# A two-layer graph network: the start laid out anew, the last eight tiles of layer 1 in a loop of their own, and q's writes and stack load moved to another sub-step

## The chip, the cores and the metric

The kernel runs on one core of a Trainium2 chip. The metric is the device time of one execution in microseconds (us); runs of the same kernel are compared by their median. Times inside the kernel come from the profile of one execution. A core has five engines that work side by side, each through its own instructions in order: TensorE (PE in the profile; its weight loads are listed as PEld), VectorE (DVE), ScalarE (ACT), GpSimd (POOL) and SyncE (SP), which here only issues DMAs. GpSimd issues DMAs too, in order with its computing.

## What is computed

x is (16, 1024, 256) in float32: 16 graphs of 1024 nodes. adj is (16, 1024, 1024) of int32, 0 or 1 in this input, about 3% ones, with ones on the diagonal. There are two layers, each with a layer norm, a ReLU and a residual:

```python
# layer 0: 8 heads of 32, D = 256
h = maximum(layernorm(x), 0)
Q, K, V = h @ Wq.T + bq, h @ Wk.T + bk, h @ Wv.T + bv      # split into heads
scores = where(adj == 0, -inf, Q K^T / sqrt(32))           # (b, head, 1024, 1024)
x = x + (softmax(scores) V) @ Wo.T + bo
# layer 1
h = maximum(layernorm(x), 0)
e_k = leaky_relu(einsum(h * a_k, h), 0.2)                  # k = 0..3
scores = where(adj == k + 1, e_k, ...), -9e15 elsewhere    # adj is 0 or 1 here: only e_0
x = x + softmax(scores) @ h
```

## The kernel before

**Tiles and steps.** The unit of work is a tile of 128 rows (nodes) of one graph; b is the graph, called a batch below, t = 0..7 the tile in it. Layer 0 handles one tile for all 8 heads in one step of the main loop (L736); step s is the pair (b, t) = divmod(s, 8). The steps overlap: in step s TensorE computes the scores of tile s (class Attend, L378), the output of tile s - 1, the projections of tile s + 9 or so (class Piece, L182, LEAD = 9 steps ahead) and layer 1 of tile s - 9 (class Edges, L547, LAG = 9 steps behind). Keys, queries and values of a graph must be whole before its first scores, and layer 1 needs all 8 tiles of a graph's layer 0, so the distances are a little over one graph. The loop ran 138 steps: 128 with scores, the last ten (s = 128 to 137) with only layer 1 and what is left of layer 0.

**The order is written out by hand** (`tc.manual_schedule()`, L699): each engine executes its instructions, and each queue its DMAs, in the order in which the program text issues them. Waits between engines are put in by the framework where a tile is written before it is read, or where its buffer is used again; work on the DRAM scratch arrays is ordered by regions in the same way. Each step has eight sub-steps h = 0..7, one per head, and the lines `if h == 3:` say which work goes where.

**One head.** Scores s = q·k (L423) are two matmuls of 128x512; VectorE adds the mask and takes the maximum (L435); ScalarE makes the Exp (L443). The probabilities must then be transposed for the product with V. Heads 2, 3, 6 and 7 are turned by TensorE (L543) and copied by ScalarE (L544). Heads 0, 1, 4 and 5 (BY_BLOCKS) go another way: VectorE transposes 32x32 blocks (L364, into the buffers "blocks"), and SP's DMAs, four of 128 KB per head, place the blocks in the turned order (L369, into "pT"). combine(0) (L478) multiplies the turned probabilities of heads 0 to 3 by V at sub-step 7, combine(1) those of heads 4 to 7 at sub-step 3 of the next step.

**Queries and keys.** Each projection (L261) is split in two halves, a high one by ScalarE (high, L277) and the remainder by VectorE (split, L282). Keys are written to a DRAM scratch array kd twice (write_keys, L309, once by SP and once by GpSimd), queries to qd (write_queries, L303: two DMAs of 256 KB on SP, which write each half twice). From there they are read back stacked, so that one matmul of full depth does the product of the halves. The query stack of one tile is one load of 512 KB into "qt" (load_queries, L390, on SP; two buffers). The key stacks are one load of 512 KB per head (load_key, L344), by SP for graph 0 and by GpSimd for the others, spread over the steps t = 7 and t = 0 at fixed places (KEY_STEPS).

**What SP's queue does in one step** of the main loop, in order: at h = 0 the first write of keys (L309) and the four placings of layer 1's tile; at h = 1 the second write of keys and the load of the next tile's stack (L390); at h = 2 and h = 3 the placings of heads 0 and 1; at h = 6 layer 1's output store (L619), the placings of head 4 and layer 0's result for later (L504); at h = 7 the placings of head 5 and q's two writes for tile s + 8 (L303).

**What GpSimd does** beside its DMAs: the mask (L403) of the next tile from adj (load L394, 512 KB, issued at h = 4), norms (norm_of, L143: a chain of 18 small operations, L152 to L168), small copies.

**Layer 1 of one tile** (Edges): scores e (L565, four matmuls of 128x512 into the score bank `sides[1]`), maximum with mask (L579), leak (L587), Exp (L591), block transposes and placings (by the same L364 and L369, into "pT1"), the product with h (gather, L609, 64 small matmuls in two halves), the store (L619). Its buffers (`sel`, `pT1`, `ha`, `x1b`) are single.

**The start.** Ahead of the loop the first graph's rows are loaded as two pieces of four tiles, normalised, turned, projected (q and k), written to qd and kd and read back, and the values computed; the first piece of graph 1 is begun. Small biases and the four weights are loaded first (L104 to L140), on SP, and each weight is turned by TensorE as it is loaded.

**After the loop** a test finds out whether some adj was over 1; then a general layer 1 (`layer_1_of_kinds`) would run. It does not run on this input.

Of the kernel before, what the change touches and what calls it, by code (L numbers as in the profile page):

```python
# [17 lines left out]
P = 128  # L18
# [24 lines left out]
def gnn_kernel(  # L43
# [59 lines left out]
    a_t = const.tile([P, NC, N_KINDS], F32, name="a_t")  # L103
    with nc.allow_non_contiguous_dma(reason="a few hundred elements, once"):  # L104
        nc.sync.dma_start(out=bq_t, in_=bq.rearrange("(c p) -> p c", p=P))
        nc.sync.dma_start(out=bk_t, in_=bk.rearrange("(c p) -> p c", p=P))
        for k, a in enumerate((a_0, a_1, a_2, a_3)):
            nc.sync.dma_start(out=a_t[:, :, k], in_=a.rearrange("(c p) o -> p (c o)", p=P))
    bv_t = const.tile([P, D], F32, name="bv_t")
    bo_t = const.tile([P, D], F32, name="bo_t")  # L110
    for i in range(2):
        nc.sync.dma_start(
            out=bv_t[:, i * P : (i + 1) * P].rearrange("p (r d) -> p r d", r=2),
            in_=bv.rearrange("(r i d) -> i r d", i=2, r=2)[i].partition_broadcast(P),
        )
    nc.sync.dma_start(out=bo_t, in_=bo.partition_broadcast(P))

    def transposed_weight(w, name):

        rows = work.tile([P, NC, D], F32, tag="p", name=f"{name}_rows", bufs=4)  # L120
        nc.sync.dma_start(out=rows, in_=w.rearrange("(c p) f -> p c f", p=P))
        wt = const.tile([P, NC, D], F32, name=name)
        tr = ps_tr.tile([P, 4, P], F32, tag="tr", name=f"{name}_tr")
        for fc in range(NC):
            for oc in range(NC):
                nc.tensor.transpose(tr[:, fc * NC + oc, :], rows[:, oc, fc * P : (fc + 1) * P], ident)
        if name == "wvT":
            for fc in range(NC):
                nc.vector.tensor_copy(
                    wt[:, fc].rearrange("p (i r d) -> p r i d", i=2, r=2),  # L130
                    tr[:, fc * NC : (fc + 1) * NC].rearrange("p r (i d) -> p r i d", i=2),
                )
        else:
            nc.vector.tensor_copy(wt.rearrange("p c f -> p (c f)"), tr.rearrange("p c f -> p (c f)"))
        return wt

    wqT = transposed_weight(wq, "wqT")
    wkT = transposed_weight(wk, "wkT")
    wvT = transposed_weight(wv, "wvT")
    woT = transposed_weight(wo, "woT")  # L140


    def norm_of(mv):  # L143
# [4 lines left out]
        def place(name, dtype=F32):  # L148
            return small.tile([P, 4], dtype, tag=name, name=name)[:, :n]

# [19 lines left out]

    def stats_place(n):
        return small.tile([P, 4, nc.vector.BN_AGGR_DIM], F32, tag="mv", name="mv")[:, :n, :]

# [5 lines left out]

    qds, kds, vs, keysets = {}, {}, {}, {}  # L180

    class Piece:  # L182
# [66 lines left out]
        def project(self, which, oc):  # L249
            wT, bias = ((wkT, bk_t), (wqT, bq_t))[which]  # L250
            b, w = self.b, self.n * P
# [67 lines left out]
        def values(self):  # L319
# [3 lines left out]
            for t in range(self.n):  # L323
                ps = (late, early, brief)[t % 3]
                self.vproj = ps
                for i, hT in enumerate((self.hTm, self.hT)):
                    for fc in range(NC):
                        nc.tensor.matmul(
                            ps[:, i * P : (i + 1) * P],
                            lhsT=hT[:, fc, t * P : (t + 1) * P],  # L330
                            rhs=wvT[:, fc, i * P : (i + 1) * P],
                            start=(fc == 0),
# [45 lines left out]
    class Attend:  # L378
# [111 lines left out]
        def output(self):  # L490
            self.y = late
            for g in range(NC):
                nc.tensor.matmul(
                    self.y, lhsT=self.oT[:, g, :], rhs=woT[:, g, :], start=(g == 0), stop=(g == NC - 1)
                )
# [195 lines left out]
    def edges_of(s):  # L691
        s -= LAG
        return Edges(*divmod(s, NT)) if 0 <= s < B * NT else None

# [4 lines left out]
    with tc.manual_schedule():  # L699
        first = [Piece(0, 0, 4), Piece(0, 4, 4)]  # L700
        piece_was = Piece(1, 0)
        for piece in (*first, piece_was):
            piece.load(nc.sync)
        for piece in (*first, piece_was):
            piece.stats()
            piece.normed()
        now, piece_next = attend_of(0), piece_of(0)
        nxt = attend_of(1)
        now.load()
        now.flag()  # L710
# [23 lines left out]

        gone = was = None
        for s in range(B * NT + LAG + 1):  # L736
            b, t = divmod(s, NT)
# [8 lines left out]
            for h in range(HEADS):  # L746
# [66 lines left out]
                if h == 1:  # L813
# [64 lines left out]
            edge_was, edge = edge, edge_nxt  # L878
            piece_was, piece = piece, piece_nxt

# [51 lines left out]
```

## Time and profile before

| | us |
|---|---|
| runs | 3287.58, 3294.10, 3294.34 |
| median of the runs | 3294.1 |
| the profiled execution | 3310.77 |
| its span, first to last instruction | 3309.0 |
| mean granted clock of TensorE in it | 0.979 |

The profiled execution is 0.5% longer than the median of the runs. Some of the costliest groups of its page, with how often each occurred and the mean time of one:

| line, engine, what | count | busy us | mean ns |
|---|---|---|---|
| L435 VectorE, mask and maximum of a head's scores | 1024 | 1233.6 | 1205 |
| L443 ScalarE, Exp | 1024 | 1178.4 | 1151 |
| L423 TensorE, scores | 2048 | 797.3 | 471 |
| L478 TensorE, probabilities times V | 16384 | 561.0 | 283 |
| L364 VectorE, block transposes | 512 | 632.2 | 1235 |
| L403 GpSimd, mask | 128 | 467.0 | 3648 |

and of its list of DMAs, with the median time from the issue to the landing:

| DMA | count | KB each | us to landing |
|---|---|---|---|
| pT from blocks, SP (L369) | 2560 | 128 | 3.5 |
| qt from qd, SP (L390) | 128 | 512 | 5.5 |
| adj, GpSimd (L394) | 127 | 512 | 4.8 |
| qd from halves, SP (L303) | 240 | 256 | 3.2 |
| k from kd, GpSimd (L344) | 120 | 512 | 7.0 |
| kd from halves, SP (L309) | 240 | 128 | 3.8 |

How to read it: busy times of matmuls overlap (matmuls are pipelined), so the mean of one is not its time alone. An arrow names what ended a wait. A line such as `1611.66 8.02 SPq L369 DMA_DIRECT2D pT<-blocks x8` of a timeline is: start in the span, length, engine or queue, line of the program, operation, output<-input, and how many instructions were put together; a bracket at its end is the wait inside it. In a row of a table by windows, the columns after the length are TensorE, its weight loads, VectorE, ScalarE, GpSimd (busy us, number of instructions), then the granted clock, the DMA engines' busy share and GB/s.

### The profile page before, as it was taken

What the parts mean: (1) busy time and instruction counts of PE and PEld (TensorE: products, weight loads), DVE (VectorE), ACT (ScalarE), POOL (GpSimd) and SP (SyncE); (2) the same over time, 40 slices, a digit from 0 to 9 for tenths busy, and PEclk for the clock granted to TensorE, in tenths of its full rate; (3) what the DMA queues carried; (4) which work ended last, traced back from release to release, by engine and by line L of the source; (5) the groups of instructions that cost most, each with busy time, mean ns of one, the idle gap of its engine ahead of it and who ended that gap; (6) DMA issues with size and microseconds to landing.
All of it is one profiled execution on the core that took longest, in us unless ns stands there. A gap on an engine that the chain in (4) does not pass through costs nothing. (4 is left out here: it accounts for less than half of the span.)

```text
span 3309.0 us, 98026 instructions
## 1 busy us (share of the span) xinstructions
PE 3080.0 (93%) x36018; PEld 2239.0 (68%) x36018; DVE 2802.7 (85%) x5111; ACT 2458.4 (74%) x4829; POOL 1735.3 (52%) x3902
## 2 busy tenths in 40 slices
PE   4888999999999999999999999999999999998997
PEld 2666767777676767767677677776766676676653
DVE  2887989989898989989899888989988899898963
ACT  2887878778787877878778777878777788787750
POOL 2555555555555555555555555555555555555531
PEclk9898999999999999999999999999999999999999
DMA  5777787877878787787878878787787877877642
GB/s 187 219 232 227 235 262 221 269 225 235 264 221 267 225 254 241 223 261 228 255 229 240 245 229 253 228 261 237 229 257 218 250 235 231 252 231 242 197 136 70
DMA packets 747063, 762.93 MB, mean 231 GB/s; under 512 B 71280, under 2 KB 692080, under 8 KB 746576
## 3 DMA queue, kind: packets, MB, share of 16 engines
q1 hardware_dynamic: 678288, 542.21, 55.3%
q0 software_dynamic: 65088, 210.16, 19.9%
q8 instruction: 290, 4.75, 0.6%
q10 hardware_dynamic: 3200, 4.19, 0.3%
q14 instruction: 197, 1.61, 0.1%
HBM read 252.98 MB, written 167.77 MB: 127 GB/s over the span
## 5 line engine op out<-in xcount | busy, mean ns | idle before, releaser
L435 DVE CUSTOM_DVE_ANT_0 p<-s,neg 128x1024 f32<-128x1024 f32 x1024 | 1233.6, 1205 | 150.6 <-issue 120.5
L443 ACT ACTIVATE p<-p,nmx 128x1024 f32<-128x1024 f32 x1024 | 1178.4, 1151 | 221.2 <-DVE nmx L435 219.7
L423 PE MATMUL s<-k,qt 128*128 128x512 f32 x2048 | 797.3, 471 | 21.8 <-DVE nmx L435 9.8
L478 PE MATMUL acc<-pT,v 128*32 128x128 f32 x16384 | 561.0, 283 | 112.3 <-DMA pT<-blocks 110.7
L544 ACT COPY pT<-trp 128x512 f32<-128x512 f32 x1024 | 543.8, 582 | 162.6 <-PE trp L543 151.9
L403 POOL TENSOR_SCALAR neg<-adj 128x1024 bf16<-128x1024 int32 x128 | 467.0, 3648 | 359.3 <-ACT neg L415 358.9
L364 DVE STREAM_TRANSPOSE blocks<-p 128x1024 f32<-128x1024 f32 x512 | 632.2, 1235 | 0.1
L478 PEld LDWEIGHTS acc<-pT,v 128*32 128x32 f32 x16384 | 472.1, 114 | 196.8 <-issue 119.4
L543 PE MATMUL trp<-ident,p 128*128 128x128 f32 x4096 | 534.2, 274 | 0.2 <-ACT pT L544 0.2
L543 PEld LDWEIGHTS trp<-ident,p 128*128 128x128 f32 x4096 | 481.0, 141 | 74.0 <-ACT pT L544 3.6
L609 PE MATMUL acc<-h,pT 128*32 128x256 f32 x8192 | 509.9, 383 | 12.5 <-DMA pT<-blocks 11.8
L565 PE MATMUL s<-h1T,ha 128*128 128x512 f32 x1024 | 482.8, 595 | 0.5 <-ACT h1T L522 0.5
L423 PEld LDWEIGHTS s<-k,qt 128*128 128x128 f32 x2048 | 331.1, 192 | 155.0 <-issue 107.7
L609 PEld LDWEIGHTS acc<-h,pT 128*32 128x32 f32 x8192 | 246.6, 110 | 228.5 <-issue 78.0
L462 POOL COPY wide<-rec 128x256 f32<-128x256 f32 x128 | 51.0, 398 | 573.3 <-DVE rec L460 573.3
L309 POOL DMA_DIRECT2D kd<-halves x240 | 169.6, 707 | 238.6 <-DVE halves L282 230.6
L579 DVE CUSTOM_DVE_ANT_0 sel<-s,neg 128x1024 f32<-128x1024 f32 x128 | 156.8, 1225 | 146.2 <-PE s L565 146.2
L565 PEld LDWEIGHTS s<-h1T,ha 128*128 128x128 f32 x1024 | 175.3, 191 | 130.0 <-issue 128.6
L591 ACT ACTIVATE sel<-sel,nmx 128x1024 f32<-128x1024 f32 x128 | 145.5, 1137 | 70.8 <-DVE rec L616 64.9
L443 ACT ACTIVATION_READ_ACCUMULATOR p<-p,nmx 128x1 f32 x1024 | 193.7, 189 | 0.0
L472 ACT COPY recT<-acc 128x256 f32<-128x256 f32 x128 | 47.8, 373 | 176.7 <-PE acc L468 176.7
L261 PEld LDWEIGHTS acc<-hT,wkT 128*128 128x128 f32 x960 | 119.5, 195 | 76.1 <-issue 46.9
(106 smaller groups left out, 4008.3 us busy)
## 6 DMA issues: line engine op xcount, KB each, us to landing
pT<-blocks SPq DMA_DIRECT2D x2560, 128.0 KB, 3.5
qt<-qd SPq DMA_DIRECT2D x128, 512.0 KB, 5.5
adj<-in_adj POOLq DMA_DIRECT2D x127, 512.0 KB, 4.8
qd<-halves SPq DMA_DIRECT2D x240, 256.0 KB, 3.2
k<-kd POOLq DMA_DIRECT2D x120, 512.0 KB, 7.0
kd<-halves SPq DMA_DIRECT2D x240, 128.0 KB, 3.8
kd<-halves POOLq DMA_DIRECT2D x240, 128.0 KB, 3.6
xb<-in_x POOLq DMA_DIRECT2D x128, 128.0 KB, 3.0
```

Of the source, the lines that this page charges most:

```text
L309: queue.dma_start(out=kds[self.b][oc, :, :, twice, self.cols], in_=halves.rearrange("p (w n) -> p w n", w=2),)
L364: nc.vector.transpose(blocks.rearrange("p b j q -> p j b q"), p)
L403: nc.gpsimd.tensor_scalar(self.neg, self.adj, 0.0, MASKED, ALU.is_equal, ALU.mult)
L423: nc.tensor.matmul(self.ps[:, cols], lhsT=self.qt[:, h, :], rhs=keysets[self.b][h][:, cols], start=True, stop=True,)
L435: nc.vector.tensor_tensor_reduce(out=p, in0=sides[h in (3, 5, 7)], in1=self.neg, scale=-SCALE, scalar=FLOOR, op0=ALU.add, op1=ALU.min, acc ...
L443: nc.scalar.activation(p, p, AF.Exp, bias=nmx, scale=-1.0, accum_out=self.sums[:, h : h + 1])
L478: nc.tensor.matmul(sums_place[r * HD : (r + 1) * HD, g * P : (g + 1) * P], lhsT=vs[self.b][:, j, place_of(h) : place_of(h) + HD], rhs=self ...
L543: nc.tensor.transpose(tr[:, j, :], p[:, jj * P : (jj + 1) * P], ident)
L544: copy(pT[:, half * 4 : half * 4 + 4, :], tr)
L565: nc.tensor.matmul(self.e[:, cols], lhsT=self.ha[:, c, :], rhs=h1Ts[self.b][:, c, cols], start=(c == 0), stop=(c == NC - 1),)
L579: nc.vector.tensor_tensor_reduce(out=self.sel, in0=self.e, in1=masks[self.b, self.t], scale=-1.0, scalar=3e38, op0=ALU.add, op1=ALU.min, a ...
L609: nc.tensor.matmul(sums_place[a * HD : (a + 1) * HD, :], lhsT=self.pT[:, j, a], rhs=h1s[self.b][:, j, :], start=(j == 0), stop=(j == NT - 1),)
```

## The change

**The start.** The rows of x are loaded first, the weights after them (in the order wk, wq, wv, wo), then the first piece of graph 1, the first adj, the biases and the next piece, all by SP. The statistics of the eight tiles of graph 0 go through one chain of norm_of (its places lie in one tile, "many", as the small tiles hold four columns). The weights are turned after the rows are normalised. All key projections of both pieces come before the query projections, and the eight key loads are issued as soon as the keys are written, ahead of q's writes and of the first stack load; the first mask and the second adj come after these. The values use the two rotating PSUM tiles of the transposes.

**The end.** The main loop ends with step 128. Layer 1's last eight tiles are computed in a loop of their own, in which both score halves of the next tile stand ahead of the gather of the tile before the one that is placed; these tiles alternate between the two score banks and use buffers that layer 0 no longer needs.

**The step.** write_queries moves from h = 7 of step s to h = 3 of step s + 1 (`piece_gone`), and load_queries of the next tile from h = 1 to h = 3, right behind it; both stay on SP. There they now stand behind the placings of head 1; before, the stack stood ahead of the placings of head 0, and q's writes behind those of head 5.

The diff, cut (the bodies of load_biases and of the weight turns are the old lines in a function; `wvT` and the like became `weights["wvT"]`):

```diff
--- before.py
+++ after.py
@@ -101,24 +101,32 @@
...
+    def load_biases():
+        with nc.allow_non_contiguous_dma(reason="a few hundred elements, once"):
+            nc.sync.dma_start(out=bq_t, in_=bq.rearrange("(c p) -> p c", p=P))
+            nc.sync.dma_start(out=bk_t, in_=bk.rearrange("(c p) -> p c", p=P))
...
+    weight_rows = {}
+
+    def load_weights():
+        for w, name in ((wk, "wkT"), (wq, "wqT"), (wv, "wvT"), (wo, "woT")):
+            weight_rows[name] = work.tile([P, NC, D], F32, tag="p", name=f"{name}_rows", bufs=4)
+            nc.sync.dma_start(out=weight_rows[name], in_=w.rearrange("(c p) f -> p c f", p=P))
+
+    def transposed_weight(name):
+
+        rows = weight_rows[name]
         wt = const.tile([P, NC, D], F32, name=name)
...
-    wqT = transposed_weight(wq, "wqT")
-    wkT = transposed_weight(wk, "wkT")
-    wvT = transposed_weight(wv, "wvT")
-    woT = transposed_weight(wo, "woT")
...
         def place(name, dtype=F32):
-            return small.tile([P, 4], dtype, tag=name, name=name)[:, :n]
+            if n <= 4:
+                return small.tile([P, 4], dtype, tag=name, name=name)[:, :n]
+            places.append(name)
+            return many[:, len(places) * n - n : len(places) * n].bitcast(dtype)
+
+        places = []
+        if n > 4:
+            many = work.tile([P, D], F32, tag="ot", name="many", bufs=1)
 
...
     def stats_place(n):
+        if n > 4:
+            return work.tile([P, n, nc.vector.BN_AGGR_DIM], F32, tag="oT", name="mv", bufs=1)
         return small.tile([P, 4, nc.vector.BN_AGGR_DIM], F32, tag="mv", name="mv")[:, :n, :]
...
         def write_queries(self):
-            for oc, halves in self.queries:
+            while self.queries:
+                oc, halves = self.queries.pop(0)
                 nc.sync.dma_start(
                     out=qds[self.b][self.first, oc].rearrange("p u w n -> p u (w n)"),
                     in_=halves.unsqueeze(1).to_broadcast([P, 2, 2 * P]),
...
             for t in range(self.n):
-                ps = (late, early, brief)[t % 3]
+                ps = late if self.n == 1 else ps_tr.tile([P, D], F32, tag="tr", name="vproj")
                 self.vproj = ps
...
-        def __init__(self, b, t):
+
+
+        def __init__(self, b, t, last=False):
             self.b, self.t = b, t
             self.rows = slice(t * P, (t + 1) * P)
+            self.side = sides[t % 2 if last else 1]
+            self.tags = {"sel": ("p", 4), "pT1": ("pT", 7)} if last else {}
+            if last and t % 2:
+                self.tags |= {"ha": ("hT", 1), "x1b": ("x1", 1)}
+
+        def buffer(self, tag, shape):
+            tag, bufs = self.tags.get(tag, (tag, 1))
+            return (ptp if tag in ("pT", "pT1") else work).tile(shape, F32, tag=tag, name=tag, bufs=bufs)
...
         def prepare(self):
-            self.ha = work.tile([P, NC, P], F32, tag="ha", bufs=1)
+            self.ha = self.buffer("ha", [P, NC, P])
...
-            self.e = sides[1]
+            self.e = self.side
...
         def softmax_max(self):
-            self.sel = work.tile([P, N], F32, tag="sel", bufs=1)
...
         def load_nodes(self):
-            self.x1 = work.tile([P, D], F32, tag="x1b", bufs=1)
+            self.x1 = self.buffer("x1b", [P, D])
...
         def place_blocks(self):
-            self.pT = placed(self.blocks, ptp.tile([P, N], F32, tag="pT1", name="pT1", bufs=1))
+            self.pT = placed(self.blocks, self.buffer("pT1", [P, N]))
...
@@ -690,7 +713,7 @@
 
     def edges_of(s):
         s -= LAG
-        return Edges(*divmod(s, NT)) if 0 <= s < B * NT else None
+        return Edges(*divmod(s, NT), s >= (B - 1) * NT) if 0 <= s < B * NT else None
...
@@ -698,42 +721,54 @@
 
     with tc.manual_schedule():
         first = [Piece(0, 0, 4), Piece(0, 4, 4)]
-        piece_was = Piece(1, 0)
-        for piece in (*first, piece_was):
+        piece_was, piece_next = Piece(1, 0), piece_of(0)
+        now, nxt = attend_of(0), attend_of(1)
+        for piece in first:
             piece.load(nc.sync)
-        for piece in (*first, piece_was):
-            piece.stats()
+        load_weights()
+        piece_was.load(nc.sync)
+        now.load()
+        load_biases()
+        piece_next.load(nc.sync)
+        mv = stats_place(NT)
+        for piece in first:
+            for t in range(piece.n):
+                stats_of(piece.x[:, t, :], mv[:, piece.first + t, :])
+        r, shift = norm_of(mv)
+        for piece in first:
+            piece.norm = tuple(a[:, piece.first : piece.first + piece.n] for a in (r, shift))
             piece.normed()
-        now, piece_next = attend_of(0), piece_of(0)
-        nxt = attend_of(1)
-        now.load()
-        now.flag()
-        now.mask()
-        nxt.load()
-        piece_next.load()
-        piece_next.stats()
+        for name in ("wkT", "wqT", "wvT", "woT"):
+            weights[name] = transposed_weight(name)
+        piece_was.stats()
         for piece in first:
             piece.turn()
-        for piece in first:
-            for which in range(2):
+        for which in range(2):
+            for piece in first:
                 for oc in range(NC):
                     piece.project(which, oc)
                     piece.high()
                     piece.split()
+            if which == 0:
+                for h in range(HEADS):
+                    load_key(0, h)
+        now.load_queries()
+        piece_was.normed()
+        now.flag()
+        now.mask()
+        nxt.load()
         for piece in first:
             piece.values()
         piece, edge, edge_was = piece_next, None, None
-        now.load_queries()
-        for h in range(HEADS):
-            load_key(0, h)
+        piece.stats()
         piece_was.turn()
         piece_was.turned()
         for oc in range(NC):
             piece_was.project(0, oc)
             piece_was.high()
 
-        gone = was = None
-        for s in range(B * NT + LAG + 1):
+        gone = was = piece_gone = None
+        for s in range(B * NT + 1):
             b, t = divmod(s, NT)
 
             def load_keys(h, end):
@@ -819,8 +854,6 @@
                         piece_nxt.load()
                     if piece_was:
                         piece_was.write_again()
-                    if nxt:
-                        nxt.load_queries()
                 if h == 2:
                     if piece_was:
                         piece_was.values()
@@ -831,7 +864,10 @@
                     if edge_was:
                         edge_was.load_nodes()
                 if h == 3:
+                    if piece_gone:
+                        piece_gone.write_queries()
                     if nxt:
+                        nxt.load_queries()
                         nxt.flag()
                         nxt.mask()
                 if h == 4:
@@ -866,8 +902,6 @@
                 if h == 7:
                     if now:
                         now.combine(0)
-                    if piece_was:
-                        piece_was.write_queries()
                     if piece:
                         piece.high()
                         piece.high()
@@ -876,7 +910,35 @@
                 load_keys(h, 1)
             gone, was, now, nxt = was, now, nxt, nxt2
             edge_was, edge = edge, edge_nxt
-            piece_was, piece = piece, piece_nxt
+            piece_gone, piece_was, piece = piece_was, piece, piece_nxt
+
+
+
+        gone.turn_normed()
+        gone.turned_normed()
+        tiles = [edge_was, edge] + [edges_of(B * NT + LAG - NT + t) for t in range(1, NT)]
+        for i in range(1, len(tiles) + 2):
+            edge = tiles[i] if i < len(tiles) else None
+            if edge:
+                edge.score(0)
+                edge.score(1)
+            if i <= len(tiles):
+                tiles[i - 1].turn_blocks()
+                tiles[i - 1].place_blocks()
+            if i >= 3:
+                tiles[i - 3].store()
+            if i >= 2:
+                tiles[i - 2].load_nodes()
+            if edge:
+                edge.softmax_max()
+                edge.leak()
+                edge.softmax_exp()
+            if i + 1 < len(tiles):
+                tiles[i + 1].prepare()
+            if i >= 2:
+                tiles[i - 2].gather(0)
+                tiles[i - 2].gather(1)
+        tiles[-1].store()
 
```

More of the change, by code (lines that the diff above doesn't have):

```diff
@@ L103, in gnn_kernel @@
     a_t = const.tile([P, NC, N_KINDS], F32, name="a_t")
[L104 to L108, printed above, removed]
     bv_t = const.tile([P, D], F32, name="bv_t")
     bo_t = const.tile([P, D], F32, name="bo_t")
[L111 to L121, printed above, removed]
+    def load_biases():
+        with nc.allow_non_contiguous_dma(reason="a few hundred elements, once"):
+            nc.sync.dma_start(out=bq_t, in_=bq.rearrange("(c p) -> p c", p=P))
+            nc.sync.dma_start(out=bk_t, in_=bk.rearrange("(c p) -> p c", p=P))
+            for k, a in enumerate((a_0, a_1, a_2, a_3)):
+                nc.sync.dma_start(out=a_t[:, :, k], in_=a.rearrange("(c p) o -> p (c o)", p=P))
+        for i in range(2):
+            nc.sync.dma_start(
+                out=bv_t[:, i * P : (i + 1) * P].rearrange("p (r d) -> p r d", r=2),
+                in_=bv.rearrange("(r i d) -> i r d", i=2, r=2)[i].partition_broadcast(P),
+            )
+        nc.sync.dma_start(out=bo_t, in_=bo.partition_broadcast(P))
+    weight_rows = {}
[5 more added lines that the diff above has]
+        rows = weight_rows[name]
         wt = const.tile([P, NC, D], F32, name=name)
@@ L177, in stats_of @@
         nc.vector.bn_aggr(out=mv, in_=st)
-    qds, kds, vs, keysets = {}, {}, {}, {}
+    qds, kds, vs, keysets, weights = {}, {}, {}, {}, {}
     class Piece:
@@ L249, in project @@
         def project(self, which, oc):
-            wT, bias = ((wkT, bk_t), (wqT, bq_t))[which]
+            wT, bias = ((weights["wkT"], bk_t), (weights["wqT"], bq_t))[which]
             b, w = self.b, self.n * P
@@ L330, in values @@
                             lhsT=hT[:, fc, t * P : (t + 1) * P],
-                            rhs=wvT[:, fc, i * P : (i + 1) * P],
+                            rhs=weights["wvT"][:, fc, i * P : (i + 1) * P],
                             start=(fc == 0),
@@ L493, in output @@
                 nc.tensor.matmul(
-                    self.y, lhsT=self.oT[:, g, :], rhs=woT[:, g, :], start=(g == 0), stop=(g == NC - 1)
+                    self.y, lhsT=self.oT[:, g, :], rhs=weights["woT"][:, g, :], start=(g == 0), stop=(g == NC - 1)
                 )
@@ L576, in softmax_max @@
         def softmax_max(self):
-            self.sel = work.tile([P, N], F32, tag="sel", bufs=1)
+            self.sel = self.buffer("sel", [P, N])
             top = small.tile([P, 1], F32, tag="top")
```

## The prediction

> **What bounds the kernel now.** I read the page's totals first, then the waits of TensorE and of SP over the even part of the run, then the timeline of one ordinary step, of one step that ends a batch, of the start and of the end.
>
> ```profile
> span 3309.0 us, 98026 instructions
> PE 3080.0 (93%) x36018; PEld 2239.0 (68%) x36018; DVE 2802.7 (85%) x5111; ACT 2458.4 (74%) x4829; POOL 1735.3 (52%) x3902
> ```
>
> TensorE is busy 93% of the span. The next view lists what TensorE waited for between 249.5 and 2986.0 us, which is steps 8 to 118 (111 steps); then comes what SP's queue waited for there.
>
> ```profile
> PE acc L478 <- DMA pT<-blocks: 100.8, 57, 6.0
> PE s L423 <- DMA k<-kd: 5.4, 8, 1.9
> ```
>
> ```profile
> SPq L369 <- DMA qt<-qd: 21.5, 20, 2.1
> ```
>
> Only one wait counts there: combine(0) (L478), for the transposed probabilities that SP's placing DMAs (L369) carry, 57 times, 100.8 us. The windows give the price of the rest: an ordinary step without the wait, the step that ends batch 7, a moment after a short wait, and all 111 steps.
>
> ```profile
> 1528.76:1551.95 23.19, 23.19 (x286) 17.13 (x283) 21.29 (x39) 18.94 (x38) 13.02 (x29) 1.00 0.75 233
> 1599.42:1630.33 30.91, 25.19 (x285) 18.72 (x282) 23.23 (x44) 20.41 (x40) 16.40 (x35) 0.89 0.90 277
> 1971.90:1975.40 3.50, 3.50 (x49) 2.82 (x39) 0.28 (x2) 0.23 (x2) 0.69 (x1) 0.51 0.65 207
> 249.50:2986.00 2736.50, 2622.62 (x31169) 1931.15 (x31167) 2421.74 (x4429) 2136.90 (x4217) 1504.33 (x3328) 0.98 0.79 240
> ```
>
> The first two columns are the window's length and TensorE's busy time. In the first window they are equal: 23.19 us is what TensorE's own work takes. 111 x 23.19 = 2574, so 162 us of the 2736.5 lie above this floor: 114 idle, 48 at a lower clock (0.89 in the second window, 0.51 in the third). Taking each step from its first score matmul (L423) in the timeline: the 13 steps t = 7 that lie between last 29.2 us on average (6.0 over the floor, 78 in all), the 14 steps t = 0 25.2 (28), the other 84 23.87 (57).
>
> Why the placing is late shows in the end of batch 7, SP first and then TensorE.
>
> ```profile
> 1611.00 0.55 SPq L390 DMA_DIRECT2D qt<-qd  x1
> 1611.66 8.02 SPq L369 DMA_DIRECT2D pT<-blocks  x8
> 1626.77 3.64 PE L478 MATMUL acc<-pT,v 128*32 128x128 f32 x62 [5.72 <-DMA pT<-blocks]
> ```
>
> The query stack (L390, 512 KB) stands ahead of the eight placings of heads 0 and 1. They take 8.02 us to issue where eight of 0.63 take 5.0: the last is held until the stack has landed (its own DMA row: 8.1 us), at 1619.1, then needs 7.4 us itself, and combine(0) waits 5.72. The 62 matmuls then take 3.64 us against 1.95 in ordinary steps.
>
> **The step's change.** Nothing is added: two q writes, 1.22 us of SP for both, and one stack load, 0.55, move behind head 1's placing. Ahead of that placing SP is thus 1.8 us freer, and the eighth DMA before the last placing is now head 0's first and not the stack. In the step from 1528.76 (times from there) VectorE ends head 1's blocks at 13.5; four placings of 0.63 then end at 16.1, q's writes at 17.4, and the stack is issued at 17.45. SP's next work is the output store (L619), which waits for VectorE until 21.1; so nothing on SP is pushed back.
>
> Gain: head 1's last placing goes out at 15.5 and lands 3.5 later (the page's median), 19.0, before combine(0) at 21.2. In an ordinary step all 0.68 go. New cost: the stack lands at 17.45 + 5.5 (median) = 22.95, and scores(0) of the next step needs it at 23.2; a slack of 0.2 that was some 7. Landings of the stack go from 4.5 to 9.8, so the step becomes max(23.19, 17.65 + landing). I keep 0.2 of the 0.68: 84 x 0.48 = 40. Bounds: 57, if it always lands within 5.5, and -10, at 6.3.
>
> The Trainium skill speaks against this move: "DMA: Bandwidth & Descriptors", section "Issuing engines are not separate DMA queues", says that transfers issued by different engines run on the same 16 DMA engines and interleave, and the mask's 512 KB load (L394) is issued by GpSimd 0.8 us before the stack. At the page's 435 GB/s these 512 KB are 1.2 us, an estimate: a landing at 6.7, a step of 24.35, and 84 x -0.5 = -40 in place of +40. The row (5.5 among other placings) is what I take, because the old place had neighbours too.
>
> At the end of a batch k's loads share the engines: landing 8.1 by the row of 1611.00, so scores(0) can start at 25.6; with 0.4 for a slower clock the step is 26.0, and 13 x 3.2 = 42 is gained, 4 more at the end of batch 14 (step 119, 30.7 us). Bounds: 20 (landing 9.8) and 69 (no wait). For the steps t = 0, which have key loads of their own, I take 0, between -14 and 28.
>
> "TensorE: Matmul & The Clock Gate", section "HAM oscillation", puts the loss of clock at idle gaps above some 3.4 us; by it the 2.4 us that stay would cost no clock, and 5 us more would be gained in all. The third window speaks against it: clock 0.51 after a wait of 2.07 us (in the step from 1947.5).
>
> q's halves now stay in their buffers until the write lands, 16.9 + 3.2 = 20.1, not 8. The next k halves are written by ScalarE at 21.9, the next q halves at 17.4. If a new tile takes the buffer released first, q gets k's (released at steps h = 0 and 1) and k gets q's, and nobody waits; cover 1.8 us. If buffers go round by creation, ScalarE waits from 17.7 to 20.1 and TensorE's projection (L261), which waits for VectorE's split, starts at 20.9 for 19.67: -1.3 a step. No view names buffers; I take the first. Sum of this part: 40 + 42 + 4 = **86** (from -30 to 150).
>
> **The start.** Before, the first score matmul starts at 78.76.
>
> ```profile
> 27.64 2.07 ACT L217 ACTIVATE pT<-pT,shift,r 128x256 f32<-128x256 f32 x4 [3.11 <-POOL shift L168]
> 42.58 0.43 DVE L176 BATCH_NORM_STATS2 st<-xin 128x6 f32<-128x256 f32 x1 [22.78 <-DMA xin<-in_x]
> 70.40 7.27 SPq L344 DMA_DIRECT2D k<-kd  x8
> ```
>
> Weights and biases come before x, two norm chains of 5.2 us follow each other on GpSimd, and VectorE stands 22.78 us for piece_next's x, whose load waits on GpSimd behind the mask; then keys are read only after all projections. Afterwards: x issued at 0.7, landed at 5 (between 2.1, the first bias, and 6.8, x behind the weights); eight statistics of 0.53, 9.3; one chain of the same 18 GpSimd operations, 14.5; eight Relu, 4.1, 18.7; the turns' last copies, 21.4; four key projections, 3.8 for the first and 2.15 each, 32; the last key write lands 5.6 later, 37.6; eight key loads issued in 7.3, 44.9; q's writes behind them, 1.2 and 6.1 to land, 52; the stack, 5.5, **58**. Weight turns, q's projections (8.6) and values (9) lie in the shadow of these DMAs. Check: kd, k and qd are 12 MB, at the 400 GB/s of this phase 31 us from 26 on: 57. Gain 78.8 - 58 = **21**; 14 if the stack needs 8.2 and the queue 4 more, 28 if q's writes overlap the key loads.
>
> **The end.** A tile of layer 1 takes 9.9 us now:
>
> ```profile
> 3247.87 3.70 PE L565 MATMUL s<-h1T,ha 128*128 128x512 f32 x8
> 3252.47 5.38 PE L609 MATMUL acc<-h,pT 128*32 128x256 f32 x64 [0.90 <-DMA pT<-blocks]
> 3257.78 3.70 PE L565 MATMUL s<-h1T,ha 128*128 128x512 f32 x8
> 3291.87 6.74 PE L609 MATMUL acc<-h,pT 128*32 128x256 f32 x64 [4.39 <-DMA pT<-blocks]
> ```
>
> The gather waits for its own placing inside the 5.38; where it doesn't wait it takes 3.72 (2 x 1.86 in ordinary steps), scores 2 x 1.72 = 3.44. In the new loop the gather comes a tile later, with two score banks and other buffers: blocks end 1.7 after a score starts, placing 4.4 later, gather at 10.6, so 4.5 of cover and 7.16 a tile. Both scores of the first tile now come after h1T's last copy (L522), at 3210.4. Eight scores and six gathers: 49.8, 3260.2. Then the last tile alone: maximum, leak and Exp 4.1, blocks 1.25, placing 4.4, gather 3.7 to 5.5 by the clock, store 0.5: 3275 where it was 3299. Gain **24** (19 to 26).
>
> **Sum.** The profiled execution took 3310.8 us: 3310.8 - 86 - 21 - 24 = 3180. The runs' median is 3294.1, 0.995 of it: **3164 us**.
>
> **Rivals.** (1) The placing isn't the stack's doing, and the move changes nothing. For it: only 20 of SP's waits name the stack, and at a batch's end k's loads stay beside the placing. Against it: L478 waits in ordinary steps too, which have no loads of k. Only start and end gain: 3310.8 - 45 = 3266, 3249 by the median. (2) The stack is somewhat late, 6.2 to 7 us: steps of 24.2, 111 x 24.2 + 13 x 2 = 2712, a gain of 24 and 45: 3242, 3225 by the median. (3) Buffers go round: 84 x -0.6, end of batch +40: -10, and 45: 3276, 3259 by the median. (4) Slower: the stack, beside the mask's load and behind q's writes in one queue, lands at 7.8 in every step, near what k's loads make of it (8.1). scores(0) waits for it and with it the whole step, 25.45: 111 x 25.45 = 2825, 88 more, less 45: 3354, **3337** by the median. It decides from a landing of 7.4 on, where 111 steps cost the 45 gained.
>
> **How the numbers follow.** Mine 0.60; (1) 0.06; (2) 0.17; (3) 0.05; (4) 0.12. My own range is 3110 to 3210. Rivals 1 to 3 reach 3259, rival 4 stays out: 3110 to 3260. A measurement here tells 0.2%, 6.6 us, from nothing. Faster 0.85, same 0.03 (edges of 1 to 3), slower 0.12.
>
> **What would show it.** L478's wait for pT gone, and the step at 23.2 to 23.7; a new wait of L423 for qt in steps t = 7. First score near 58. Gathers 7.2 us apart at the end. I am wrong if L423 waits for qt in ordinary steps, or if ScalarE's q halves (L277) wait for qd.

## The result and the profile after

The changed kernel is slower: a median of 3388.96 us over four runs (3382.5 to 3401.01) against 3294.22 us, a ratio of 1.0292 (95% interval 1.0252 to 1.0331). The range ended at 3260; what happened is the rival on the other side, the stack that lands late in every step.

The page of the changed kernel, its totals first, then the rows of its list of DMAs with the median time to landing:

```profile
span 3399.1 us, 97636 instructions
PE 3073.9 (90%) x36018; PEld 2240.7 (66%) x36018; DVE 2816.1 (83%) x5111; ACT 2462.2 (72%) x4829; POOL 1725.6 (51%) x3883
...
pT<-blocks SPq DMA_DIRECT2D x2560, 128.0 KB, 2.9
qt<-qd SPq DMA_DIRECT2D x128, 512.0 KB, 6.9
adj<-in_adj POOLq DMA_DIRECT2D x127, 512.0 KB, 5.5
qd<-halves SPq DMA_DIRECT2D x240, 256.0 KB, 5.7
```

TensorE is busy for as many microseconds as before (3074 against 3080), but over 90 us more. The placings land sooner (2.9 for 3.5), the stack later (6.9 for 5.5), q's writes much later (5.7 for 3.2). In the new file the scores are L436, P times V L491, the stack's load L403, q's writes L316, adj's load L407, the high halves L289, the placings L382, layer 1's product L632.

What TensorE waited for between 244.9 and 3093.3 us, steps 8 to 118 (line, what for, us, times, longest), and then the same for ScalarE:

```profile
PE s L436 <- DMA qt<-qd: 210.9, 112, 8.2
PE s L436 <- DMA k<-kd: 6.9, 9, 1.7
```

```profile
ACT halves L289 <- DMA qd<-halves: 131.2, 138, 4.5
```

The wait of combine(0) for the placing (100.8 us before) has left the list; in its place the next step's scores wait 210.9 us for the stack, in every step: 1.36 us on average at the end of the steps t = 1 to 6, 4.95 at the end of t = 7, 2.03 at the end of t = 0. In the steps t = 1 to 6 this replaces 0.42 us on average that combine(0) waited before. ScalarE has a new wait, for q's writes. Where the 90 us between the two spans lie (for the steps by t the mean, and in the last column the sum):

| stretch | before | after | difference |
|---|---|---|---|
| start to the first score | 78.8 | 66.2 | -12.5 |
| steps 0 to 7 | 170.7 | 178.7 | +8.0 |
| steps 8 to 118 | 2736.5 | 2848.3 | +111.8 |
| of it 84 steps t = 1 to 6, mean | 23.86 | 24.81 | +80 |
| 13 steps t = 7, mean | 29.18 | 28.35 | -11 |
| 14 steps t = 0, mean | 25.21 | 28.26 | +43 |
| steps 119 to 126 | 182.9 | 186.4 | +3.5 |
| step 127 to the end | 140.1 | 119.4 | -20.7 |

The timeline of one ordinary step, which began at 2453.58, shows how it comes about (start, length, engine or queue; SP, then GpSimd, then TensorE):

```profile
2464.23 5.79 SPq L382 DMA_DIRECT2D pT<-blocks  x8
2470.07 1.29 SPq L316 DMA_DIRECT2D qd<-halves  x2
2471.40 1.55 SPq L403 DMA_DIRECT2D qt<-qd  x1
...
2470.23 0.59 POOL L407 DMA_DIRECT2D adj<-in_adj  x1
...
2478.32 0.73 PE L436 MATMUL s<-k,qt 128*128 128x512 f32 x2 [1.49 <-DMA qt<-qd]
```

Within 1.4 us q's two writes, adj and the stack are issued, 1.5 MB. The stack lands at 2478.28, 6.88 after its issue, and the next step begins at once. The table by windows, for the stretch of 6.5 us that begins 16.5 into an ordinary step (length, five engines, granted clock, DMA engines' busy share, GB/s), first of the kernel before, then of the changed one:

```profile
1545.26:1551.76 6.50, 6.50 (x122) 4.41 (x114) 6.19 (x14) 5.99 (x14) 4.94 (x21) 1.00 0.50 161
```

```profile
2470.08:2476.58 6.50, 6.50 (x122) 4.41 (x114) 6.19 (x14) 5.39 (x12) 4.94 (x21) 1.00 0.93 261
```

The DMA engines were half idle there and are now busy to 93%, moving 261 GB/s. Over all 84 ordinary steps (t = 1 to 6) the share in this stretch went from 0.60 to 0.91, at 264 GB/s.

### The profile page after: what moved, and what is told of

Its sections match the earlier page's. It is cut to its first block, busy times and chain, and to the rows that moved or that the text cites. A ratio compares the mean times of both kernels' runs of the same rounds, so it can differ in the third digit from the quotient of the medians.

```text
span 3399.1 us, 97636 instructions
## 1 busy us (share of the span) xinstructions
PE 3073.9 (90%) x36018; PEld 2240.7 (66%) x36018; DVE 2816.1 (83%) x5111; ACT 2462.2 (72%) x4829; POOL 1725.6 (51%) x3883
## 3 DMA queue, kind: packets, MB, share of 16 engines
q0 software_dynamic: 65040, 210.03, 20.1%
## 5 line engine op out<-in xcount | busy, mean ns | idle before, releaser
L436 PE MATMUL s<-k,qt 128*128 128x512 f32 x2048 | 802.3, 474 | 261.2 <-DMA qt<-qd 235.3
L377 DVE STREAM_TRANSPOSE blocks<-p 128x1024 f32<-128x1024 f32 x520 | 642.1, 1235 | 11.1 <-ACT p L614 10.8
L436 PEld LDWEIGHTS s<-k,qt 128*128 128x128 f32 x2048 | 333.1, 193 | 399.4 <-DMA qt<-qd 182.3
L556 PE MATMUL trp<-ident,p 128*128 128x128 f32 x4096 | 554.1, 280 | 0.2 <-ACT pT L557 0.2
L556 PEld LDWEIGHTS trp<-ident,p 128*128 128x128 f32 x4096 | 497.6, 145 | 74.9 <-issue 4.6
L491 PE MATMUL acc<-pT,v 128*32 128x128 f32 x16384 | 517.7, 276 | 3.5 <-DMA pT<-blocks 2.7
L632 PE MATMUL acc<-h,pT 128*32 128x256 f32 x8192 | 494.7, 383 | 3.3 <-DVE ot L641 3.3
L491 PEld LDWEIGHTS acc<-pT,v 128*32 128x32 f32 x16384 | 445.8, 111 | 73.3 <-DVE ot L641 38.6
L588 PE MATMUL s<-h1T,ha 128*128 128x512 f32 x992 | 490.1, 619 | 0.0
L632 PEld LDWEIGHTS acc<-h,pT 128*32 128x32 f32 x8192 | 242.4, 110 | 206.9 <-issue 57.3
L602 DVE CUSTOM_DVE_ANT_0 sel<-s,neg 128x1024 f32<-128x1024 f32 x120 | 146.9, 1224 | 126.7 <-PE s L588 126.7
L289 ACT ACTIVATE halves<-acc,bk_t 128x128 fp32r<-128x128 f32 x240 | 86.3, 362 | 142.8 <-DMA qd<-halves 139.6
L294 DVE SCALAR_TENSOR_TENSOR halves<-acc,bk_t,halves 128x128 fp32r<-128x128 f32 x240 | 80.3, 335 | 109.8 <-PE acc L531 75.6
```

Of the source, the lines that this page charges most:

```text
L377: nc.vector.transpose(blocks.rearrange("p b j q -> p j b q"), p)
L436: nc.tensor.matmul(self.ps[:, cols], lhsT=self.qt[:, h, :], rhs=keysets[self.b][h][:, cols], start=True, stop=True,)
L491: nc.tensor.matmul(sums_place[r * HD : (r + 1) * HD, g * P : (g + 1) * P], lhsT=vs[self.b][:, j, place_of(h) : place_of(h) + HD], rhs=self ...
L556: nc.tensor.transpose(tr[:, j, :], p[:, jj * P : (jj + 1) * P], ident)
L588: nc.tensor.matmul(self.e[:, cols], lhsT=self.ha[:, c, :], rhs=h1Ts[self.b][:, c, cols], start=(c == 0), stop=(c == NC - 1),)
L602: nc.vector.tensor_tensor_reduce(out=self.sel, in0=self.e, in1=masks[self.b, self.t], scale=-1.0, scalar=3e38, op0=ALU.add, op1=ALU.min, a ...
```

## The experiments: what makes the stack late

Each run is compared with the kernel before on the same chip, whose median there was 3304.5 for the first four runs below, 3301.4 for adj's load two sub-steps later, the stack at h = 0, the start in another order and these last two edits together, and 3288.8 for the three runs with a fifth buffer and for the best kernel with adj later. So runs of different chips are compared by their ratios to the kernel before. Lists of waits are over steps 8 to 118. Theory A: q's writes, ahead of the stack in SP's queue. Theory B: the place, where q's writes, adj and the stack share the DMA engines. Theory C: the buffers of the halves, for which ScalarE waits. Theory D: the start or the end.

**Start and end alone** (the stack back at h = 1, q's writes at h = 7).

```diff
 # h == 1
+                    if nxt:
+                        nxt.load_queries()
 # h == 3
-                    if piece_gone:
-                        piece_gone.write_queries()
-                        nxt.load_queries()
 # h == 7
+                    if piece_was:
+                        piece_was.write_queries()
```

> The new start and the new end, with the stack and q's writes back in their old places. In the trace of the changed kernel the first score comes 12.5 us earlier and the stretch from step 127 to the end is 20.7 us shorter. Theory A (the whole loss lies in the step): before less 33, about 3261 (3255 to 3268), with the ordinary step back at 23.9 and the wait of combine(0) for pT back. Theory D (start or end disturb the even part too, by other buffers): 3290 or more, with ordinary steps above 24.2.

Measured 3269.3 us, ratio 0.9893 (0.9857 to 0.993). First score at 66.4, step 127 to the end 119.1 us, ordinary steps 23.89, and combine(0)'s wait for the placings is back (90.9 us). Theory D falls: start and end gain 35 us together, and the loss is all in the step.

**The stack alone moved** (q's writes back at h = 7, in the lines shown above).

> As the changed kernel, but q's writes stay at h = 7 of their own step; only the stack moves to h = 3. Theory A (q's two writes, 512 KB ahead of the stack in SP's queue, are what makes it late: they take 1.4 us to issue and 1.2 of its landing): the stack is issued at 16.6 and lands 5.5 later, at 22.1, ordinary steps 23.3 to 23.5, no wait for qt in them, steps t = 7 and t = 0 some 26: about 3200. Theory B (the place itself, beside the mask's load of adj): landing 6.5 or more, at 23.2, ordinary steps 23.6 to 23.8, t = 7 and t = 0 27.5: about 3240.

Measured 3228.9, ratio 0.9757 (0.9726 to 0.9788): faster. Its waits of TensorE over steps 8 to 118:

```profile
PE s L436 <- DMA qt<-qd: 48.8, 25, 4.8
PE acc L491 <- DMA pT<-blocks: 29.3, 37, 2.2
```

The stack is issued at 17.1 and lands at 22.85 on average, 5.73 later, 0.3 before the scores need it: ordinary steps 23.65, t = 7 26.6, t = 0 25.9. This is near what the prediction had forecast of the stack for the whole change (a landing of 5.5, t = 7 at 26.0), though ordinary steps gain 0.2 us here where 0.48 was forecast, and the total lies above the forecast 3164.

**q's writes alone moved** (the stack back at h = 1).

> As the changed kernel, but the stack stays at h = 1; only q's writes move to h = 3 of the next step. Theory A: q's writes alone hinder nobody; about as the kernel with only start and end new, 3255 to 3275, ScalarE's wait for qd under 0.4 us a step. Theory C (q's halves are now the buffers that k's halves need, and ScalarE's wait of 1.2 us a step for qd is on the path): slower than that kernel by 40 or more, 3300 to 3390, with ScalarE's wait for qd near 1 us a step.

Measured 3224.6, ratio 0.9742 (0.9711 to 0.9773): faster by as much again, which no theory had expected. TensorE's waits, then ScalarE's:

```profile
PE acc L491 <- DMA pT<-blocks: 30.2, 19, 4.8
PE acc L491 <- issue: 30.0, 9, 4.9
```

```profile
ACT halves L289 <- DMA qd<-halves: 164.5, 170, 5.7
```

With q's writes (issued at 4.8 and 5.4 in the run with start and end alone) gone from the first half of the step, the stack goes out at 9.4 and not 10.5 as there, the placings behind it follow, and ordinary steps take 23.51. ScalarE waits for q's writes more than in the changed kernel, and the step doesn't notice. So each half of the move gains some 40 us beyond start and end, and both together lose some 4% (a ratio of 1.0292 against 0.9893).

**The stack ahead of q's writes.**

```diff
                 if h == 3:
+                    if nxt:
+                        nxt.load_queries()
                     if piece_gone:
                         piece_gone.write_queries()
                     if nxt:
-                        nxt.load_queries()
                         nxt.flag()
```

> As the changed kernel, but at h = 3 the stack is loaded ahead of q's writes. Theory A: the stack is issued at 16.6, lands within 5.9, at 22.5; ordinary steps 23.3 to 23.6; about 3210. Theory B: landing 6.5 or more all the same, steps 23.7; about 3240. Theory C: q's writes land 0.8 later than in the changed kernel, ScalarE waits 2 us a step for qd and steps stay above 24.3: 3330 or more.

Measured 3279.3, ratio 0.9918 (0.9887 to 0.9949). The stack is issued at 17.0 and lands 6.46 later, though nothing of SP's stands right ahead of it any more: theory A in its narrow form falls, the order in the queue gives back 1.0 us of issue and only 0.3 of landing. The wait for qt falls to 0.28 us in ordinary steps, yet they take 24.02. ScalarE waits for q's writes, which now land at 24.6 and 25.3.

**adj's load two sub-steps later.**

```diff
 # h == 4
-                    if nxt2:
-                        nxt2.load()
 # h == 6, behind now.load_nodes()
+                    if nxt2:
+                        nxt2.load()
```

> As the changed kernel, but GpSimd issues the load of the next adj (512 KB) at h = 6 and no longer at h = 4, that is not beside q's writes and the stack. Theory A (q's writes in front of the stack in SP's queue are the cause): the stack still lands 6.4 or more after its issue at 18.0, ordinary steps 24.4 or more, total 3345 to 3390. Theory B (the three of 512 KB, q's writes, adj and stack, share the same engines in the same 6 us; each taken away frees as much): landing 5.7, ordinary steps 23.7, total 3270 to 3310.

Measured 3221.5, ratio 0.9760 (0.9729 to 0.9791), some 5% under the changed kernel by the two ratios, from one load of GpSimd that the change had not touched. The waits of TensorE, the rows of the list of DMAs, and the same 6.5 us of an ordinary step by windows:

```profile
PE s L436 <- DMA qt<-qd: 58.1, 31, 5.3
```

```profile
qt<-qd SPq DMA_DIRECT2D x128, 512.0 KB, 4.6
...
qd<-halves SPq DMA_DIRECT2D x240, 256.0 KB, 3.3
```

```profile
2434.90:2441.40 6.50, 6.50 (x120) 4.43 (x114) 6.18 (x14) 5.98 (x14) 4.43 (x20) 1.00 0.75 219
```

SP's order is the same, the stack still goes out at 18.07; it lands 4.63 later in place of 6.75, and q's writes take 3.2 and 3.5 in place of 4.7 and 5.8. Theory B holds, and its price was set too low. Ordinary steps 23.33, the end of t = 7 still waits 3.4 for the stack.

**A fifth buffer for the halves**, in the changed kernel and in the one with the stack first.

```diff
-            bufs = {"p": 4, "blocks": 3, "halves": 4, "qt": 2, "xin": 2}.get(tag, 1)
+            bufs = {"p": 4, "blocks": 3, "halves": 5, "qt": 2, "xin": 2}.get(tag, 1)
```

> The changed kernel with five buffers for halves in place of four, so that k's halves need not wait for q's writes. Theory C (buffers go round to k's halves, and ScalarE's wait of 1.2 us a step is part of the loss): ScalarE's wait gone and ordinary steps down from 24.8 to 24.0: 3290 to 3320. Theory B (the stack's landing alone sets the step, the buffers cost nothing): ScalarE's wait gone as well, the stack still landing 6.7 after its issue, ordinary steps 24.6 to 24.9: 3370 to 3395.

Measured 3404.4, ratio 1.0359 (1.0328 to 1.039). ScalarE's waits, then TensorE's:

```profile
ACT halves L289 <- DMA qd<-halves: 24.5, 27, 2.4
```

```profile
PE s L436 <- DMA qt<-qd: 201.7, 110, 10.0
```

ScalarE's wait is gone but for a fifth, and nothing is gained: theory C falls for the changed kernel. The wait that sets the step is the stack's.

> The kernel with the stack ahead of q's writes, with five buffers for halves. There the stack landed at 23.5, yet ordinary steps took 24.0 and ScalarE waited 2 us a step for qd. Theory C for this kernel: with the fifth buffer ordinary steps fall to 23.5 to 23.6, total 3225 to 3245, near the kernel that moves the stack alone (3229). If the buffers are not it: 3270 to 3285.

Measured 3227.4, ratio 0.9829 (0.9782 to 0.9875), ordinary steps 23.57 against 24.02. There the missing fifth buffer costs some 0.9% by the two ratios. How is not shown: ScalarE's wait for q's writes did not go (221 us between 240 and 2919 with four buffers, 240 with five). What fell is VectorE's wait for ScalarE's halves, from 149 to 67 us, and the stack went out at 16.5 and landed at 23.0, each 0.5 sooner. A quarter-microsecond wait for qt stays (0.24).

## The experiments: a better place, and the start

**The stack at h = 0**, with q's writes at h = 3.

```diff
                 if h == 0:
+                    if nxt:
+                        nxt.load_queries()
                     if piece_was:
                         piece_was.write_again()
```

> q's writes at h = 3 of the next step as in the changed kernel, the stack at h = 0 in front of all placings of heads 0 and 1. If the placings of heads 0 and 1 are late only where the stack is issued among them: combine(0) no longer waits in ordinary steps (23.2 to 23.3) and its wait at t = 7 falls from 3.0 to under 1.5: 3175 to 3200, against 3225 with the stack at h = 1. If any early stack delays them (the slots of SP's DMAs or the engines' share are used up all the same): 3215 to 3235.

Measured 3208.6, ratio 0.9722 (0.9688 to 0.9756), between the two cases. Steps t = 7 fall from 27.4 to 25.0, ordinary ones from 23.51 to 23.40, but steps t = 0 rise from 25.8 to 27.6: most of what one end of the batch gains the other gives back. By its interval the total isn't told apart from the kernel with the stack at h = 1 (0.9742).

**The start in another order**, in the kernel with q's writes alone moved: q's writes ahead of the key loads, and these as key 0, stack, keys 1 to 7.

```diff
-            if which == 0:
-                for h in range(HEADS):
-                    load_key(0, h)
+        load_key(0, 0)
         now.load_queries()
+        for h in range(1, HEADS):
+            load_key(0, h)
```

> As the kernel with only q's writes moved, and in the start q's writes go out before the key loads, which follow as key 0, stack, keys 1 to 7. If the first score waits because q's writes and the stack stand behind eight key loads (4 MB) in SP's queue: first score at 53 to 57 in place of 66.4, total 3213 to 3218. If the start is bound by the sum of its DMAs: first score at 63 or later, total 3221 to 3228.

TensorE's timeline:

```profile
55.91 1.19 PE L436 MATMUL s<-k,qt 128*128 128x512 f32 x2 [4.08 <-DMA qt<-qd]
```

The first score stands at 55.9, 10.5 us earlier: the order of the queue held it, not the sum of the DMAs. The total, 3213.9 (0.9744, 0.9706 to 0.9782), isn't told apart from the kernel without this edit (0.9742).

> The last two edits together: the sum of their gains, 3165 to 3190 if both hold; 3215 or more if neither does.

Measured 3191.6, ratio 0.9671 (0.9643 to 0.9698), the fastest here, some 6% below the changed kernel by the two ratios; the gain is somewhat under what was expected. Its page:

```profile
span 3190.4 us, 97828 instructions
...
PE 3048.5 (96%) x36018; PEld 2217.1 (69%) x36018; DVE 2794.3 (88%) x5111; ACT 2442.7 (77%) x4829; POOL 1726.8 (54%) x3883
```

Two further edits of this kernel gave nothing more.

> The kernel with both edits (stack at h = 0, start's order) and adj's load at h = 6 as well. If what is left above the floor comes from q's writes and adj sharing the engines (q's halves come free late, ScalarE waits 1 us a step for qd): ScalarE's wait for qd falls to 0.3 us a step, steps t = 0 from 27.5 to 26, total 3165 to 3180 against 3192. If adj at h = 6 collides with the placings of heads 4 and 5 instead: 3190 or more.

Measured 3192.8, ratio 0.9705 (0.9676 to 0.9734). Steps t = 0 fall from 27.5 to 26.5, but t = 7 rise from 24.1 to 25.6.

> The kernel with both edits (stack at h = 0, start's order), with five buffers for halves. If ScalarE's wait for qd (1 us a step) is what makes steps t = 0 long there: 27.5 falls to 26, total 3165 to 3180. If k's loads alone make them long: 3188 to 3195.

Measured 3191.9, ratio 0.9705 (0.9679 to 0.9731). ScalarE's wait is half gone (116 to 54 us; in a step t = 0 from 3.7 to 2.1), and steps t = 0 stay at 27.5. So the part of the wait that went did not make these long. Whether the rest of it does, or k's loads, is open; moving k's loads was not tried.

## Why the prediction was wrong

- **The wait removed: right.** combine(0)'s 100.8 us are gone (the page's row for L491 has 2.7 left over the whole span), as the new place of the stack was to bring.
- **The step's length as 17.65 + landing: right in form.** Measured issue 18.0, landing 6.75, sum 24.77; measured step 24.81. The issue came 0.55 after the forecast 17.45: head 1's placings, put at 16.1 from four of 0.63 behind VectorE's 13.5 in one step, were done at 16.5 on average, and q's writes went out at 16.6 and 17.3. The 0.2 between 17.45 and 17.65 has no row behind it; from landing to the first score it took 0.04. Nor does the lower bound of -30 for this part follow from its own bounds, which add up to -10 + 20 - 14 = -4.
- **The step that failed** is "The row (5.5 among other placings) is what I take, because the old place had neighbours too". The neighbours were counted as present or absent, not in bytes. At the old place they are placings of 128 KB each; at the new one 1 MB is issued in the 1.4 us ahead of the stack. The engines' share alone doesn't tell the places apart: at the old one it was 0.88 from 10.6 to 16.0 of the ordinary steps of before, while the stack landed. Taking adj away makes the landing 4.63, taking q's writes away 5.73, both left in 6.75: adj costs 2.1 us, q's writes 1.0 and another 0.9 of issue. With any one of the three gone from this place (adj, the stack or q's writes) the kernel takes some 5% less than the changed one (0.9760, 0.9742 and 0.9757 against 1.0292).
- **The rule set aside would have come nearer.** The Trainium skill, "DMA: Bandwidth & Descriptors", section "Issuing engines are not separate DMA queues", says that transfers of different issuers share the 16 engines; the run with adj later shows it, with GpSimd's load costing SP's stack 2.1 us. The estimate made from it, a landing at 6.7, was met to 0.1, but partly by luck: it priced adj at 435 GB/s, 1.2 us, while the engines moved 264 GB/s there, and left q's writes out. At 264, 1.5 MB from 16.6 on take 6.0 us, and with 2.1 more, the median landing of layer 1's output store in the kernel before, the stack comes at 24.7; with 1 MB, 22.7. Measured: 24.8 with all three, 22.85 and 22.70 with two. This sum was made after the runs and is a fit, not a rule that they show: with 1 MB the engines moved 241 and 227 GB/s on average in the 6.5 us stretch, not 264.
- **Ends of a batch.** The landing of 8.1 was carried over too; it was 10.1, the step 28.35 where 26.0 was forecast, and 11 us came in for 42. Steps t = 0 were put at nothing, between -14 and 28 gained; they lost 43: there the stack goes out at 20.1 and takes 8.1.
- **Rival 4 was the mechanism**, with its price mis-sized in shape: 25.45 in every step was forecast, 24.8 in ordinary steps and 28.3 at both ends of a batch were measured, 112 us in place of 88. It got 0.12 because the row with the old neighbours was held to be the evidence, and a rule with a number was held to be the guess.
- **The buffers of q's halves.** The picture was right (the halves that wait are k's, as q's buffers come to them), the cover of 1.8 us was not: it went with a landing of 3.2, and the writes took 4.7 and 5.8. ScalarE waits 1.2 us a step, which costs nothing beside the later stack: the fifth buffer took four fifths of it away there and gained nothing.
- **The start: 12.5 for 21.** Right: one norm chain, key loads issued from 37.4 on (37.6 forecast). Mis-sized: "q's writes behind them, 1.2 and 6.1 to land".

```profile
37.44 9.16 SPq L357 DMA_DIRECT2D k<-kd  x8
51.08 5.72 SPq L306 DMA_DIRECT2D qd<-p  x4
61.47 0.36 SPq L403 DMA_DIRECT2D qt<-qd  x1
```

  In this timeline of SP q's writes go out at 51.1, not 44.9, take 5.7 us to issue, and 8 to 11 us to land; the stack goes at 61.5 where 52 was forecast. The sum left out that ScalarE issues the other half of q's writes, from 36.8 to 44.7, beside the key loads: these took 6.6 to 15.6 us to land, and SP's first and fourth write each went out just after one of them had landed (51.0 and 56.4). The check by the sum of bytes missed it, as it asks how long the engines need and not what stands last in the queue.
- **The end: 20.7 for 24.** TensorE's timeline has the gathers 7.2 us apart, as forecast, and where the rest went:

```profile
3319.64 0.69 PE L531 MATMUL acc<-ident,h 128*128 128x128 f32 x2 [3.32 <-ACT h L524]
3320.12 6.20 PE L588 MATMUL s<-h1T,ha 128*128 128x512 f32 x8
3326.15 3.60 PE L588 MATMUL s<-h1T,hT 128*128 128x512 f32 x8
...
3344.44 3.66 PE L632 MATMUL acc<-h,pT 128*32 128x256 f32 x64
...
3351.66 3.66 PE L632 MATMUL acc<-h,pT 128*32 128x256 f32 x64
...
3379.30 5.35 PE L632 MATMUL acc<-h,pT 128*32 128x256 f32 x64 [2.31 <-DVE ot L641]
```

  The first eight score matmuls take 6.20 in place of 3.60 after a wait of 3.3 us (the granted clock is 0.57 from 3319.6 to 3326.3), and the gather before the last waits 2.31 us and then takes 5.35 in place of 3.66, at a clock of 0.68.

## What to carry to other kernels

When a transfer is moved, add up the bytes that all queues issue in the microseconds around its new place, and set them against the rate that the trace shows; the landing of 5.5 us measured at the old place was 6.75 at the new one. A move that groups several transfers at one point can turn two gains into a loss, so its parts are worth trying alone. At the start the first score waited for what stood last in the queue, not for the sum of its bytes.

## What the runs showed of the hardware

The DMA engines were nearly full at 261 to 264 GB/s (busy share 0.91 to 0.93) with this mix of transfers, while the start, with its own mix, moved 365 GB/s at a share of 0.98 between 27.5 and 66 us: the rate at which the engines are nearly full differs with the transfers. A DMA issued later in SP's own queue can slow one issued earlier: the stack ahead of q's writes landed in 6.46 us, and in 5.73 with q's writes away at h = 7. After a wait of TensorE of 2.31 us the granted clock was 0.68 over the next 5.4 us.
